# One GAT layer of a six-layer graph network: its last, half-wide block multiplied in the usual way, a mask fetched behind a transposing DMA, and sums of values made over three blocks

## The chip, the cores and the metric

The kernel runs on one core of a Trainium2 chip. The metric is the device time of one execution in microseconds; the median of several runs is compared. A time below 2259.1 us would be faster by more than 0.3%.

## What is computed

A graph of N = 3327 nodes with D = 256 features goes through four residual layers, each `x = layernorm(x + gnn(x, adj))`. The last of them is itself three graph-attention (GAT) layers in a row, so the kernel makes six passes over the graph, named "0", "1", "2", "3a", "3b" and "3c". The change is in layer "1" and where layer "0" passes into it. Cut to what matters:

```python
def gat(x, adj, W, a):                       # layer 1
    h = x @ W
    e = (h @ a[:D, 0])[:, None] + (h @ a[D:, 0])[None, :]
    e = where(e > 0, e, 0.01 * e)
    att = softmax(where(adj > 0, e, -1e12), axis=1)
    return elu(att @ h)

x = layernorm(x + cosine_attention(x, adj))      # layer 0
x = layernorm(x + gat(x, adj, W, a))             # layer 1
x = layernorm(x + dot_attention(x, adj))         # layer 2
x = layernorm(x + gat3(x, adj))                  # layer 3: 3a, 3b, 3c
```

All arithmetic is in float32; `adj` is 0 or 1, about one entry in a hundred, and is turned into a byte mask once.

## The kernel before

**Tiles and blocks.** The nodes are padded to 3328 = 26 tiles of 128 (NT = 26). The target nodes of a pass are cut into seven blocks (NB = 7): six of 512 and a last one, block 6, of 256. In a pass the kernel runs over the blocks `b`, and in a block over the 26 source tiles `j`. For each `(b, j)` it makes the weights `e` (128 source nodes x 512 or 256 targets): ScalarE (ACT) computes a rectified form `re` (L788, four buffers, so that the `re` four tiles on waits until `e` has read this one), and VectorE (DVE) multiplies it with the mask and writes `e` (L801, nine buffers, which the sums named below share). TensorE (PE) then multiplies `e` with the values `v` of tile `j`, which carry a column of ones, so that the sum of weights comes out with the product.

**Two ways to multiply.** The usual way is `plain` (L912 to L919): for each 128 target nodes one product 128 x 257 per source tile, accumulated in a PSUM bank. The other way takes two source tiles as a pair `p` (13 pairs) and two column tiles, and makes seven half-wide products instead of eight, Strassen's scheme in Winograd's form. It needs sums of the weights, `half_sums` (DVE, L901 to L904, four operations for a pair), and sums of the values, `tsums`. In layer 1 block 0 is all plain; in a block for which `half(L, b)` holds, column tiles 2 and 3 are plain and 0 and 1 go through `half_products` (L937); at the end `half_joined` (L953 to L963) puts the seven accumulators together. Block 6 has two column tiles only, and there all products are `half_products`.

**Sums of values.** They don't depend on the block. `combine(key, p, v)` (L837 to L860) makes them for one pair, once a layer: a column of ones by GpSimd (L850), four DVE operations (L851, L852, L858, L859), and a write to DRAM, `t_d` (L860). For each block and pair `fetch_tsum` (L864) brings 256.5 KB back; the buffers, shared by `combine` and `fetch_tsum`, are three. The 13 pairs of layer 1 are made in layer 0's block 6 and in layer 1's blocks 0 and 1, at steps `j` written out by hand; pair 12 is made when its values are done.

**The end of a block.** `finish(L, b, pos)` (L1187) normalizes the accumulators into `p4` (`ri` by DVE L1285 and L1286, the scaling by ACT L1271; for the columns of `half_joined` after the join), turns `p4` and projects it with W, adds the residual and normalizes to `o`. A second turn, of the `o` of the block before, gives the transposed features `ft` that the next layer needs. Both go through `turn` (L1063 to L1081), a generator that runs beside the next block's products: two ACT copies to `planes` (L1070), a transposing DMA on SyncE (SP; L1073), and, some steps later, two copies from `turned` to the place wanted (L1080). So in layer 1 each block has two turns: first `ft`'s, at the block's start, then `p4`'s.

**What sets the order.** The layers are written as a stream of steps, and the framework's scheduler arranges the instructions of each engine for itself, within the data dependences and buffers; the only order asked for by hand is `tc.issue_after(instruction)`, which makes what is issued inside wait in order behind that instruction. SP issues the loads and stores, and its transfers share one queue on 16 DMA engines. In that queue are the mask of the next block (`fetch_mask`, L425 to L428, 1664 KB, or 832 KB for block 6; two buffers; asked for at `j == 8`), the `tsums`, the `t_d` writes of the next layer's pairs, the turns and the rows `x_d` of the residual.

## Time and profile before

| | |
|---|---|
| median of 3 runs | 2265.93 us (2261.41 to 2267.34) |
| profiled execution | 2268.84 us, its span 2266.9 us |
| granted TensorE clock, mean | 0.995 |
| PE busy | 2225.6 us, 98% |
| DVE busy | 2011.5 us, 89% |
| ACT busy | 1360.4 us, 60% |
| layer 1's products, block 0 to 6 | from 466 to about 811 us |
| `tsums<-t_d` fetches in the execution | 230 of 256.5 KB |
| `mask<-mask_d` fetches | 30 of 1664 KB (the page's size; the last block's is half) |

Times in the views are microseconds from the start of the span. An engine's row gives busy time and, in the views of waits, what ended its idle time: `PE po L937 <- DMA tsums<-t_d` reads "PE's product at line 937 waited for the transfer of `tsums`". A matmul in float32 shows as two records. The start of the next record of a filled PE comes 0.111 us after a 128-column one and 0.217 us after a 257-column one; where it comes later, PE stalled. The granted clock is what the throttle gave TensorE, 1.00 being full speed.

### The profile page before, as it was taken

What the parts mean: (1) busy time and instruction counts of PE and PEld (TensorE: products, weight loads), DVE (VectorE), ACT (ScalarE), POOL (GpSimd) and SP (SyncE); (2) the same over time, 40 slices, a digit from 0 to 9 for tenths busy, and PEclk for the clock granted to TensorE, in tenths of its full rate; (3) what the DMA queues carried; (4) which work ended last, traced back from release to release, by engine and by line L of the source; (5) the groups of instructions that cost most, each with busy time, mean ns of one, the idle gap of its engine ahead of it and who ended that gap; (6) DMA issues with size and microseconds to landing.
All of it is one profiled execution on the core that took longest, in us unless ns stands there. A gap on an engine that the chain in (4) does not pass through costs nothing.

```text
span 2266.9 us, 43735 instructions
## 1 busy us (share of the span) xinstructions
PE 2225.6 (98%) x15801; PEld 2034.4 (90%) x15801; DVE 2011.5 (89%) x5682; ACT 1360.4 (60%) x2315; POOL 90.9 (4%) x269
## 2 busy tenths in 40 slices
PE   9999999999999899999999999999999999999997
PEld 7788888888989879999999999999999999999997
DVE  7789999978888788988998879999899998899997
ACT  4677777766666534444444445666666665666663
POOL 0000001000000000000000000000000010000000
PEclk9999999999999999999999999999999999999999
DMA  8655655645665642223222254556536556355542
GB/s 283 196 177 169 196 191 190 188 140 133 156 155 136 157 117 82 62 92 91 61 96 72 75 145 146 158 152 162 141 117 163 147 150 166 100 160 160 152 121 57
DMA packets 207964, 318.05 MB, mean 140 GB/s; under 512 B 82829, under 2 KB 115588, under 8 KB 203140
## 3 DMA queue, kind: packets, MB, share of 16 engines
q1 hardware_dynamic: 198836, 307.12, 46.7%
q0 software_dynamic: 8640, 7.87, 2.3%
q8 instruction: 125, 2.05, 0.4%
q14 instruction: 91, 0.75, 0.1%
q10 hardware_dynamic: 272, 0.26, 0.0%
HBM read 248.69 MB, written 41.85 MB: 128 GB/s over the span
## 4 chain that ended last, share of the span: by engine, by line
PE 84%; DVE 7%; DMA 4%; ACT 2%; issue 2%; POOL 0%; SPq 0%; DVEq 0%; ACTq 0%; POOLq 0%
PE po L1016 46%; PE ps L650 10%; PE po L914 9%; PE ps L511 6%; PE po L937 4%; PE pproj L1336 3%; PE ps L687 2%; DVE ft L801 1%; DMA tsums<-t3a_d 1%; PE pv L1434 1%; PE pgq L541 1%; PE pproj L1131 1%; ACT re L788 1%; DMA turned<-planes 1%; PE pk L371 1%
## 5 line engine op out<-in xcount | busy, mean ns | idle before, releaser
L788 ACT ACTIVATE re<-u,nrh,th 128x512 f32<-128x512 f32 (+1 forms) x728 | 534.1, 777 | 220.7 <-DVE ft L801 120.0
L1016 PE MATMUL po<-tsums,qsum 128*128 128x128 f32 (+1 forms) x2520 | 352.4, 276 | 6.3 <-DMA tsums<-t3a_d 1.9
L801 DVE SCALAR_TENSOR_TENSOR ft<-re,rh,mask 128x512 f32<-128x512 f32 x468 | 338.5, 742 | 5.9 <-ACT re L788 5.9
L1016 PEld LDWEIGHTS po<-tsums,qsum 128*128 128x128 f32 x2520 | 315.9, 192 | 8.4 <-issue 3.5
L1016 PE MATMUL po<-tsums,ssum 128*128 128x128 f32 (+1 forms) x2082 | 316.6, 275 | 2.4 <-DVE ssum L892 1.0
L1016 PEld LDWEIGHTS po<-tsums,ssum 128*128 128x128 f32 x2082 | 286.7, 192 | 16.9 <-issue 5.0
L914 PE MATMUL po<-v,e 128*128 128x257 f32 x1248 | 294.9, 381 | 0.8 <-DVE e L525 0.6
L1016 PE MATMUL po<-v,ft 128*128 128x129 f32 x1872 | 286.3, 276 | 0.7 <-DVE ft L801 0.6
L914 PEld LDWEIGHTS po<-v,e 128*128 128x128 f32 x1248 | 229.8, 190 | 38.4 <-issue 7.9
L1016 PEld LDWEIGHTS po<-v,ft 128*128 128x128 f32 x1872 | 252.1, 192 | 5.2 <-DVE ft L801 1.3
L1016 PEld LDWEIGHTS po<-v,e 128*128 128x128 f32 x1196 | 170.1, 191 | 35.9 <-issue 23.7
L801 DVE SCALAR_TENSOR_TENSOR e<-re,rh,mask 128x512 f32<-128x512 f32 (+1 forms) x234 | 151.2, 655 | 40.8 <-PE po L937 17.7
L524 ACT ACTIVATE ex<-ps,rq 128x512 f32<-128x512 f32 (+1 forms) x183 | 118.9, 652 | 114.0 <-PE ps L511 108.9
L1016 PE MATMUL po<-v,e 128*128 128x129 f32 x1196 | 183.1, 275 | 0.0
L496 DVE SCALAR_TENSOR_TENSOR e<-ex,mask 128x512 f32<-128x512 f32 (+1 forms) x182 | 118.1, 650 | 57.0 <-ACT ex L673 30.4
L511 PE MATMUL ps<-ft 128*128 128x512 f32 (+1 forms) x364 | 167.1, 564 | 0.1
L1016 PE MATMUL po<-tsums,ft 128*128 128x128 f32 x936 | 143.4, 276 | 0.1
L525 DVE SCALAR_TENSOR_TENSOR e<-ex,mask 128x512 f32<-128x512 f32 (+1 forms) x183 | 116.0, 641 | 25.4 <-ACT ex L524 24.8
L1016 PE MATMUL po<-v,qsum 128*128 128x128 f32 x840 | 128.6, 276 | 0.0
L1016 PEld LDWEIGHTS po<-tsums,ft 128*128 128x128 f32 x936 | 123.9, 193 | 0.3 <-ACT p L1271 0.3
L467 DVE CUSTOM_DVE_ANT_0 acc<-acc,stage 128x1024 uint16<-128x1024 uint16 (+1 forms) x168 | 108.3, 645 | 12.2 <-DMA stage<-in_adj_a 9.9
L650 PE MATMUL ps<-gsums,ksum 128*128 128x256 f32 x408 | 111.3, 380 | 0.0
(374 smaller groups left out, 4122.5 us busy)
## 6 DMA issues: line engine op xcount, KB each, us to landing
tsums<-t_d SPq DMA_DIRECT2D x230, 256.5 KB
mask<-mask_d SPq DMA_DIRECT2D x30, 1664.0 KB
stage<-in_adj_a SPq DMA_DIRECT2D x78, 512.0 KB
tsums<-t3a_d SPq DMA_DIRECT2D x77, 256.5 KB
tsums<-t3b_d SPq DMA_DIRECT2D x77, 256.5 KB
tsums<-t3c_d SPq DMA_DIRECT2D x77, 256.5 KB
t_d<-tsums SPq DMA_DIRECT2D x39, 256.5 KB
mask_d<-mask SPq DMA_DIRECT2D x6, 1664.0 KB
```

The costliest lines, as they stand in the source:

```text
L467: nc.vector.tensor_tensor(acc, acc, st[:, h * wd : (h + 1) * wd], ALU.add)
L496: nc.vector.scalar_tensor_tensor(e[:, :wd], t_[:, :wd], 0.0, mask(b, j), ALU.add, ALU.mult)
L511: nc.tensor.matmul(ps[:, :wd], FT[j // 4][:, 0, (j % 4) * P : (j % 4 + 1) * P], FT[b][:, 1, :wd], start=True, stop=True,)
L524: nc.scalar.activation(t_[:, c], ps[:, c], AF.Exp, scale=rq[:, j : j + 1])
L525: nc.vector.scalar_tensor_tensor(e[:, c], t_[:, c], 0.0, mask(b, j)[:, c], ALU.add, ALU.mult)
L650: nc.tensor.matmul(out, l, r, start=first, stop=True, skip_group_check=True)
L788: nc.scalar.activation(t_[:, :wd], self.u[b][:, :wd], AF.Relu, bias=self.nrh[:, j : j + 1], scale=self.th[:, j : j + 1],)
L801: nc.vector.scalar_tensor_tensor(e[:, :wd], t_[:, :wd], self.rh[:, j : j + 1], mask(b, j), ALU.add, ALU.mult,)
L914: nc.tensor.matmul(pos[k - k0], e[:, k * P : (k + 1) * P], v[i], start=(i == 0), stop=(i == NT - 1),)
L937: nc.tensor.matmul(pos[g][:, c : c + n], *m[k], start=(p == 0 and k in (1, 7)), stop=(p == NT // 2 - 1 and k in (5, 3)),)
L1016: nc.tensor.matmul(o, x, y, start=(p == 0 and g not in banks[:i]), stop=(p == NT // 2 - 1 and g not in banks[i + 1 :]),)
L1336: nc.tensor.matmul(pm[:, :D], pT[:, h, :], w[L.w][:, h, :], start=(h == 0), stop=(h == 1),)
```

## The change

It has three parts. `half` no longer holds for block 6, so that its products are plain, 26 tiles x 2 column tiles, without `half_sums`, `tsums` or `half_joined`. `turn` remembers its last transposing DMA, and in layer 1, for blocks 2 to 6, the mask of the next block is issued behind it on SP. And the `combine`s of layer 1's pairs are placed anew: before, pairs 0 to 4 in layer 0's block 6 (at j = 5, 10, 15, 20, 25), 5 to 9 in layer 1's block 0 (j = 1, 5, 9, 13, 17), and 10 and 11 in block 1 (j = 1, 5); after, pairs 0 to 2 in layer 0's block 6 (j = 6, 12, 18), 3 to 8 in block 0 (j = 1 to 21 by four), and 9 to 11 in block 1 (j = 1, 5, 9).

```diff
     def half(L, b):
-        return L.key == "1" and b > 0
+        return L.key == "1" and 0 < b < NB - 1
...
+    last_turn = [None]
+
     def turn(x4, n, out, steps=3, copy=nc.vector.tensor_copy):
...
         tr = work.tile([P, 16, P], U16, tag="stage", name="turned", bufs=4)
-        nc.sync.dma_start_transpose(
+        last_turn[0] = nc.sync.dma_start_transpose(
             out=tr[:, : 4 * n, :], in_=pl[:, :n].rearrange("p k t n -> p (k t n)")
         )
...
         elif j == 8 and not (last and b == NB - 1):
             nb = (b + 1) % NB
-            masks[nb] = fetch_mask(nb)
+            if L.key == "1" and b > 1:
+                with tc.issue_after(last_turn[0].ins):
+                    masks[nb] = fetch_mask(nb)
+            else:
+                masks[nb] = fetch_mask(nb)
...
-        if L.key == "0" and b == NB - 1 and j % 5 == 0 and j > 0:
-            combine("1", j // 5 - 1, V[1])
-        if L.key == "1" and j % 4 == 1 and j < (20, 8, 0, 0, 0, 0, 0)[b]:
-            combine("1", (5 if b == 0 else 10) + j // 4, V[1])
+        if L.key == "0" and b == NB - 1 and j % 6 == 0 and 0 < j < 24:
+            combine("1", j // 6 - 1, V[1])
+        if L.key == "1" and j % 4 == 1 and j < (24, 12, 0, 0, 0, 0, 0)[b]:
+            combine("1", (3 if b == 0 else 9) + j // 4, V[1])
```

## The prediction

> **What bounds the kernel now.** The page comes first: what is busy, and on which line the chain that ended last runs.

> ```profile
> PE 2225.6 (98%) x15801; PEld 2034.4 (90%) x15801; DVE 2011.5 (89%) x5682; ACT 1360.4 (60%) x2315; POOL 90.9 (4%) x269
> PE 84%; DVE 7%; DMA 4%; ACT 2%; issue 2%; POOL 0%; SPq 0%; DVEq 0%; ACTq 0%; POOLq 0%
> ```

> TensorE (PE) is the bound; only its work and its stalls count. The table by stages says where it stalls. Its rows are layer 0's block 6, then layer 1's blocks 0 to 6; after each window and its length stands PE's busy time, and the number after the last engine is the granted clock.

> ```profile
> 432.80:466.00 33.20, 32.30 (x146) 26.57 (x145) 31.02 (x130) 26.13 (x57) 1.07 (x8) 1.00 0.54 181
> 466.00:514.50 48.50, 48.50 (x226) 42.04 (x227) 35.41 (x102) 30.42 (x47) 0.41 (x2) 1.00 0.44 123
> 514.50:559.80 45.30, 45.30 (x312) 42.58 (x311) 37.66 (x117) 31.90 (x49) 0.10 (x1) 1.00 0.49 134
> 559.80:611.40 51.60, 49.71 (x333) 46.30 (x332) 44.12 (x145) 34.61 (x52) 3.95 (x6) 1.00 0.66 157
> 611.40:662.10 50.70, 49.69 (x332) 46.29 (x331) 44.04 (x144) 34.64 (x52) 3.62 (x6) 1.00 0.65 158
> 662.10:714.50 52.40, 49.72 (x333) 46.31 (x332) 44.43 (x148) 34.02 (x49) 3.65 (x6) 1.00 0.58 139
> 714.50:765.60 51.10, 49.88 (x332) 46.14 (x331) 43.01 (x147) 33.55 (x54) 3.65 (x6) 1.00 0.59 149
> 765.60:810.70 45.10, 38.08 (x235) 32.71 (x235) 34.97 (x142) 20.00 (x34) 4.20 (x6) 0.92 0.62 156
> ```

> Blocks 0 and 1 stall nowhere. Blocks 2 to 5 have one gap each of 1 to 3 us, block 6 has 7.0 us and a clock of 0.92. The view of waits over layer 1's blocks 1 to 6 names what ended them (total, times, longest):

> ```profile
> PE po L937 <- DMA tsums<-t_d: 7.3, 5, 2.7
> PE po L937 <- DVE ft L1080: 2.9, 1, 2.9
> PE po L937 <- DVE e L801: 2.6, 1, 2.6
> ```

> A seven-product group at a block's start waits for its sums (`tsums`). The SyncE queue at the start of block 2 (559.8) shows why they are late:

> ```profile
> 552.80 0.38 SPq L427 DMA_DIRECT2D mask<-mask_d  x1
> 554.78 5.02 SPq L1073 DMA_TRANSPOSE turned<-planes  x1
> 559.89 6.52 SPq L864 DMA_DIRECT2D tsums<-t_d  x4
> 567.50 1.85 SPq L1073 DMA_TRANSPOSE turned<-planes  x1
> ```

> The turn of the normalized rows (554.78) stands behind 1664 KB of mask, holds SP for 5.02 us (1.85 where no mask is ahead), and `tsums` is issued only after it. Summing PE's start-to-start excess over its steady pitch gives the stalls: 2.16, 1.27, 2.95 and 1.71 us in blocks 2 to 5, 8.1 together. In block 6 they are 3.02, 1.63, 2.75 and 0.28, 7.7 together, and two of them are followed by half clock (third number before the end 0.51 and 0.53):

> ```profile
> 769.10:772.00 2.90, 2.89 (x13) 2.90 (x14) 1.17 (x5) 2.87 (x5) 0.00 (x0) 0.51 0.36 137
> 789.50:792.60 3.10, 3.04 (x13) 2.95 (x14) 0.16 (x1) 0.00 (x0) 0.00 (x0) 0.53 0.78 195
> ```

> They lose 2.90 x 0.49 + 3.10 x 0.47 = 2.9 us. Block 6 thus has 7.7 + 2.9 = 10.6 us to win, blocks 2 to 5 have 8.1.

> **Block 6 plain.** Removed: 13 pairs x 7 products x 2 records at 0.111 us pitch, 20.3 us. Added: 26 tiles x 2 columns x 2 records at 0.2166, 22.5 us (pitches of L937 and L914). PE +2.3. DVE loses 13 x 4 `hsum` operations at 0.2 us pitch, 10 us of the 34.97 above, off the path. SP loses 13 `tsums` fetches, and with them the waits for their landing, all 10.6 us. What is late next: the first product waits for `e` (0.4, an estimate from DVE's queue at 764 to 766); the projections of block 5 stand after 21 plain products and 8 of `pv`, 21 x 0.433 + 8 x 0.433 = 12.6 us, while the turn they need comes 5.9 us after its planes (772.17 to about 778 in this block), which end about S + 8 (S: the block's first PE product), so about 1.1; the norms 0.3. Together 1.8; bounds 0 (planes as early as now, S + 6.5) and 4.1 (the two largest waits of ACT's `pT` and DVE's `psums` for a turn, 2.1 and 2.0). Sum: -10.6 + 2.3 + 1.8 = -6.5 (-8.3 to -4.2).

> The clock row needs a reason, since other stalls cost none: block 2's 2.06 us and block 4's 2.85 were followed by full clock, 3.02 and 2.75 by half. So I charge nothing for new stalls up to 2.1 us, and 1.45 (half of 2.9) for each of 3 us or more. [...]

> **The mask behind the turn (blocks 2 to 5).** In the built order of the changed kernel SP now has: x_d writes, `tsums` of pair 0, turn, `tsums` 1 to 3, the second turn, mask, write of a `combine`d pair of the next layer (`t_d`, L860), `tsums` 4. The first turn has no mask ahead: its copies can start about 4.4 us after its planes (567.46 to 571.82 in block 2). Planes end at 554.75, S - 5.05; so the turned rows are there at S - 0.65, not S + 3.5 as now. The `tsums` stall goes.

> But the scheduler uses this: the two `ft` copies (L1080; ACT 1.34, DVE 0.75) now stand ahead of `ri` (DVE, L1285) and of the two `p<-po` scalings (ACT, L1271) that free PE's accumulators of the block before. Now these run at S - 1.5 to S - 0.2. By hand through the new order: ACT's sixth `re` waits for DVE's `e` of tile 3 (four buffers); `ft` on ACT runs S + 0.65 to S + 1.9; DVE has `ri` at S + 1.6; the first scaling ends at S + 2.35. The plain columns of the new block queue behind it on PE, and the whole PE queue with them: a stall of about 2.0, and 0.2 for the join (L961). Bounds: 0 if DVE's `e` runs a little earlier and `ft` fits in, 2.95 by the largest block-start stall of the trace.

> The later cost: the second turn's planes end at S + 10.3, its packets run S + 11.3 to 14.05, the mask then needs 5.4 us (packets 553.7 to 559.0 in block 2), to S + 19.4; the `t_d` write and `tsums` 4 stand behind it and land at S + 21.7. PE needs them at S + 21.0: 0.8 stall in blocks 2 to 4 (0 to 3.7), none in block 5, whose next mask is half as large. After: 3 x 3.0 + 2.1 = 11.1 against 8.1: +3.0 (bounds -8.1, all stalls gone, and +7).

> The rule against this move is on the record of layer 2: a mask issued at 896.79 held back the write issued at 897.22 until 904.1. So what stands behind a mask on this queue pays for it; the 0.8 above has it in.

> **Sums over three blocks.** The built order has one `combine` fewer on DVE in layer 0's block 6, and two later ones in layer 1's blocks 0 and 1. One is 4 operations, 0.82 us of DVE. In layer 0 PE's own excess is 2.06 us, and DVE waits 1.01 there for a `tsums` buffer: -0.5 (0 to -0.8). In blocks 0 and 1 DVE has 13.1 us free in 48.5 and PE no stall: 0. If that cover were gone, 2 x 0.82 = 1.6.

> **Sum.** -6.5 + 3.0 - 0.5 = -4.0. The profiled execution took 2268.84 (span 2266.9), 2.9 above the median of 2265.93; the difference carries over: 2264.8 in a profile like that one, **2261.9** as a median.

> **The rivals.**
> *A, the stalls really go.* The `ft` copies find their data ready and cost the path nothing, since the `e` that ACT waits for comes early enough. For: the turn lands before S; DVE is busy 44 of 51 us, so it has room. Against: four copies at the block's narrowest place. The start stalls, 3 x 2.2 + 2.1 = 8.7 us of my 11.1, are gone: 2253.2.
> *B, the mask stalls the middle of the blocks.* One mechanism: in blocks 2 to 4 the planes of the second turn end about 3 us later than S + 10.3 (they queue on ACT behind `re`, which waits for `e`: the 63.1 us of ACT's waits for DVE are mostly that). The mask follows the turn, and `tsums` 4 the mask: stall 3.7, not 0.8. That is 3 x 2.9 = 8.7 more, and half clock after two of three, 2.9: 2273.5 (2270.6 without the clock). It decides from the point where the planes end after S + 12. For: 0.7 us of margin in my chain is the wrong way already. Against: today the planes end at S + 7.7.
> *C, the wait only changes its place.* Whatever is gained at the start is lost to `ri` and the scalings in equal measure; blocks 2 to 5 keep 8.1, the rest holds: 2258.9.

> **How the numbers follow.** Forecast 0.52, own range 2256 to 2267 (its block-start stalls between 0.7 and 3.3 each); A 0.24, B 0.15, C 0.09. 0.3% of 2265.93, about what a measurement of this kernel can tell from no change, is 6.8 us: below 2259.1 or above 2272.7. Faster: 0.3 of the forecast, all of A, half of C: 0.16 + 0.24 + 0.04 = 0.44. Slower: 0.7 of B and 0.02 of the forecast, 0.12. Same 0.44. The range from 2251 to 2272 leaves out the best of A, where everything of the 8.1 goes, and the upper part of B: under 0.2.

> **What would show it.** Block 6: no PE wait for `tsums`, clock 1.00, first product of layer 2 at S + 42 (48.5 now); if it is above S + 44.5, the first term is wrong. Blocks 2 to 5: SP's first turn under 3 us, no mask ahead of it; PE stalled about 2 us at the start by ACT L1271 (two lines further down in the changed file), not by DMA; if that is under 0.5, A. PE's wait for `tsums` at S + 21: 0.8; above 3, B, with rows of half clock. A stall in blocks 0 and 1 would make the last part wrong, and so would a median outside 2251 to 2272.

## The result, and the profile after

The changed kernel takes 2276.86 us (median of 6 runs, 2273.48 to 2282.32) against 2265.39 for the kernel before: a ratio of 1.0052, 95% interval 1.0034 to 1.0070. It is slower by some 11 us; 2261.9 was forecast, and the time lies above the range. The profiled execution took 2274.62 us, one of the changed kernel's faster ones.

The page first: the rows that answer to the two of before.

```profile
PE 2228.3 (98%) x15723; PEld 2030.3 (89%) x15723; DVE 2000.7 (88%) x5623; ACT 1357.2 (60%) x2314; POOL 90.7 (4%) x269
PE 79%; DVE 8%; DMA 8%; ACT 3%; issue 2%; POOL 0%; SPq 0%; DVEq 0%; POOLq 0%; ACTq 0%
```

PE's work is nearly what it was (+2.7 us; +2.3 was forecast for the plain block). But DMA has 8% of the chain that ended last, where it had 4%. The table by stages (layer 0's block 6, then layer 1's blocks 0, 2, 3, 4, 5 and 6) looks for the loss where the change was made:

```profile
432.80:467.10 34.30, 33.18 (x156) 27.61 (x155) 31.01 (x131) 25.73 (x56) 1.17 (x9) 1.00 0.52 168
467.10:515.60 48.50, 48.50 (x226) 41.82 (x225) 35.31 (x101) 30.78 (x47) 0.41 (x2) 1.00 0.45 130
...
561.00:614.00 53.00, 49.88 (x327) 45.61 (x326) 44.18 (x146) 35.00 (x52) 3.96 (x6) 1.00 0.58 152
614.00:666.50 52.50, 50.65 (x338) 46.84 (x338) 43.69 (x145) 34.61 (x52) 3.63 (x6) 1.00 0.57 149
666.50:720.70 54.20, 50.64 (x333) 46.37 (x332) 44.77 (x151) 34.44 (x52) 3.65 (x6) 1.00 0.57 150
720.70:772.30 51.60, 49.60 (x329) 45.61 (x328) 41.89 (x139) 33.58 (x53) 3.84 (x8) 1.00 0.52 125
772.30:811.00 38.70, 37.81 (x159) 29.29 (x158) 28.04 (x104) 19.08 (x35) 3.44 (x4) 1.00 0.66 174
```

Blocks 2 to 5 became longer (53.0, 52.5, 54.2, 51.6 against 51.6, 50.7, 52.4, 51.1). Block 6 lost its gaps and its half clock: 38.7 us at 1.00 instead of 45.1 at 0.92. The two cancel: the first score product of layer 2 starts at 805.6 us, 805.7 before, and layer 2's last score product starts at 1357.7 in both. **The 6 us by which this execution is longer lie behind 1357.7, in layers 3a to 3c and the end of the program, where every engine has the same instructions in the same order.** The stretch from layer 2's last score product to PE's last product is 902.3 us, 896.2 before. What PE waited for in it (total, times, longest), first before, then after:

```profile
PE po L1016 <- DMA tsums<-t3a_d: 1.9, 3, 1.3
...
PE pproj L1336 <- DVE zlast L1511: 1.3, 1, 1.3
PE po L1016 <- DMA tsums<-t3c_d: 1.2, 1, 1.2
...
PE po L1016 <- DMA tsums<-t3b_d: 0.7, 1, 0.7
```

```profile
PE po L1016 <- DMA tsums<-t3a_d: 4.0, 5, 1.7
PE po L1016 <- DMA tsums<-t3b_d: 2.8, 4, 1.7
PE pproj L1338 <- DVE zlast L1513: 2.8, 1, 2.8
...
PE po L1016 <- DMA tsums<-t3c_d: 1.2, 1, 1.2
```

So fetches of value sums in layer 3 land late in a part of the program that was not touched: 8.0 us of waiting for them instead of 3.8. They are not all of it. The piece behind the last product with value sums takes 35.0 us instead of 31.9: there PE waits 2.8 us instead of 1.3 for the last turn (`zlast`), and 3.4 us at half clock follow. That piece is longer (32.9 to 35.0 us against 31.7 to 31.9) in each profile whose stretch is 899 us or more, but for one (r9); how the late fetches lead to it was not traced. The experiments had to tell whether that was chance, and if not, what carries an edit of layer 1 into layer 3.

### The profile page after: what moved, and what is told of

Same layout as the page of the kernel before. It is cut to its first block, busy times and chain, and to the rows that moved or that the text cites. A ratio compares the mean times of both kernels' runs of the same rounds, so it can differ in the third digit from the quotient of the medians.

```text
span 2272.8 us, 43505 instructions
## 1 busy us (share of the span) xinstructions
PE 2228.3 (98%) x15723; PEld 2030.3 (89%) x15723; DVE 2000.7 (88%) x5623; ACT 1357.2 (60%) x2314; POOL 90.7 (4%) x269
## 4 chain that ended last, share of the span: by engine, by line
PE 79%; DVE 8%; DMA 8%; ACT 3%; issue 2%; POOL 0%; SPq 0%; DVEq 0%; POOLq 0%; ACTq 0%
PE po L1016 43%; PE ps L650 10%; PE po L914 9%; PE ps L511 6%; PE pproj L1338 3%; PE po L937 2%; DMA turned<-planes 2%; PE ps L687 2%; DMA tsums<-t3a_d 1%; DMA tsums<-t3b_d 1%; DVE ft L801 1%; DMA tsums<-t_d 1%; PE pgq L541 1%; PE pv L1436 1%; ACT planes L1072 1%
## 5 line engine op out<-in xcount | busy, mean ns | idle before, releaser
L801 DVE SCALAR_TENSOR_TENSOR ft<-re,rh,mask 128x512 f32<-128x512 f32 x468 | 338.7, 742 | 19.2 <-ACT re L788 19.1
L914 PE MATMUL po<-v,e 128*128 128x257 f32 x1352 | 320.4, 381 | 2.9 <-ACT p L1273 2.1
L914 PEld LDWEIGHTS po<-v,e 128*128 128x128 f32 x1352 | 248.9, 190 | 46.3 <-issue 9.8
L1016 PEld LDWEIGHTS po<-v,e 128*128 128x128 f32 x1196 | 170.1, 191 | 36.1 <-issue 23.4
L801 DVE SCALAR_TENSOR_TENSOR e<-re,rh,mask 128x512 f32<-128x512 f32 (+1 forms) x234 | 151.2, 656 | 33.4 <-PE po L937 12.6
L467 DVE CUSTOM_DVE_ANT_0 acc<-acc,stage 128x1024 uint16<-128x1024 uint16 (+1 forms) x168 | 108.4, 645 | 13.2 <-DMA stage<-in_adj_a 11.5
```

The source lines that it names most:

```text
L467: nc.vector.tensor_tensor(acc, acc, st[:, h * wd : (h + 1) * wd], ALU.add)
L801: nc.vector.scalar_tensor_tensor(e[:, :wd], t_[:, :wd], self.rh[:, j : j + 1], mask(b, j), ALU.add, ALU.mult,)
L914: nc.tensor.matmul(pos[k - k0], e[:, k * P : (k + 1) * P], v[i], start=(i == 0), stop=(i == NT - 1),)
L1016: nc.tensor.matmul(o, x, y, start=(p == 0 and g not in banks[:i]), stop=(p == NT // 2 - 1 and g not in banks[i + 1 :]),)
```

## The experiments

Each was timed in five rounds beside the kernel before. "Stretch" is always the time from layer 2's last score product to PE's last product; PE's waits are given as its start-to-start excess over its steady pitch.

**r1: the change once more.** No edit.

> The changed kernel once more, for a second profile. In the first one the end of layer 1 (the first score product of layer 2, ps<-gT,ft) came at 805.6 us, as before (805.7), and the 6 us lost came in layers 3a to 3c, after 1357 us, which the change doesn't touch. Theory 'chance': the stretch behind layer 1 differs by several us between executions of one program; this profile will show it at another length, and the loss in the median must then sit in layer 1 for the most part. Theory 'shifted': something the change leaves behind (13 transfers fewer, another rotation of buffers) makes the stretch from 1357 us to the end longer in every execution: again about 896 to 897 us from the first score product of layer 2's last stretch to the last projection, against 890 before.

Measured: 2278.29 us, ratio 1.0050 (1.0035 to 1.0065). Its profile is of an execution of 2271.01 us, the fastest of six; layer 2 begins at 805.1 and the stretch is 899.2, halfway between 896.2 and 902.3 (the lengths in the expectation are of a shorter piece). The loss of the median is steady, so it isn't chance. Two profiled executions that are both faster than their median can't tell where the rest of it lies; the parts alone can.

**r2, r3, r4: the three parts alone**, each a hunk of the diff on the kernel before.

> Block 6 plain alone, mask and sums as before. Layer 1: blocks 2 to 5 keep their stalls of 8.1 us, block 6 loses its stalls and half clock: first product of layer 2 about 6.5 us earlier (bounds 4.2 to 8.3). If the rest is untouched, ratio about 0.997. Theory 'shifted': the stretch behind layer 1 is 6 us longer here too, since the 13 transfers are gone, and the ratio is about 1.000.

> The mask behind the second turn alone. Theory 'mask' (rival B, smaller): each of blocks 2 to 4 loses about 2 to 3 us to tsums of pairs 4 and 5 behind the mask and 1 to 1.5 at its start, in place of 1.3 to 2.95 before; blocks 2 to 5 together 4 to 6 us longer; block 6, whose first turn has no mask ahead, 2 to 3 us shorter; ratio 1.001 to 1.002. Theory 'shifted' with the loss tied to the mask's order: ratio 1.004 to 1.006, the surplus behind 1357 us.

> The sums of values over three blocks alone. By my sum -0.5 us; by the profile of the changed kernel, where layer 0's block 6 ended no earlier, 0 to +0.5. Ratio 1.000 within 0.001. A ratio above 1.003 would mean that the later write of pair sums is on the path somewhere.

Measured: block 6 plain 2273.22 us, ratio **1.0031** (1.0019 to 1.0043). The mask 2271.98, **1.0028** (1.0019 to 1.0037). The sums 2265.64, 1.0000 (0.9992 to 1.0009).

The sums cost and bring nothing. The mask by itself loses 3.6 us by the first score product of layer 2 (809.3 against 805.7), and its stretch, 895.7, is that of before; the median loses 6.3, more than the 1.001 to 1.002 that was expected. Its waits are not quite those of the whole change, though: its block 6, still with seven-product groups, was expected to be 2 to 3 us shorter and has a stall of 5.6 us of its own (PE's products waiting for DVE's `e`) and 6.8 us at half clock, which the plain block doesn't have.

The plain block is the surprise. Layer 2 begins at 801.2, 4.5 us earlier, at the low end of the forecast's 4.2 to 8.3; and the kernel is 7 us slower, since the stretch is 907.0 instead of 896.2. So the edit that wins in layer 1 loses twice as much in layer 3. PE's waits there:

```profile
PE po L1016 <- DMA tsums<-t3a_d: 7.2, 4, 2.2
...
PE po L1016 <- DMA tsums<-t3c_d: 2.4, 3, 1.2
PE po L1016 <- DMA tsums<-t3b_d: 2.3, 1, 2.3
```

**What differs in layer 3?** The order is the same. Fetch by fetch (231 of them), mostly the same ones are slow in r1, r2 and the changed kernel, and others in the three kernels that keep their half products in block 6 (the fetches' times correlate at 0.75 to 0.83 among the first three, at 0.67 to 0.75 among the others, at 0.34 to 0.43 across). The queues on the page give the clue, before and after:

```profile
q8 instruction: 125, 2.05, 0.4%
```

```profile
q8 instruction: 124, 2.03, 0.4%
```

This is a queue for instructions: 125 packets, 2.05 MB together, 16 KB each, each 1.07 us long in the median (0.96 in the changed kernel). PE ran 15801 products and as many weight loads; with its 416 other records, nearly all waits, that is 32018, or 256 per packet, and the median number of PE's records between two packets is 256 too. So these are pages of PE's program, 256 instructions each. The plain block takes away 39 products of four instructions each and some waits, 164 in all (168 in the whole change). All later page ends are thereby moved by 164 instructions against the work. That gives a theory, 'pages', and a rival, 'buffers': 13 fetches fewer also rotate the three `tsums` buffers.

Counted over layer 3, 27 of the 231 fetches overlap a page's packet in the kernel before (29 in r4, 33 in r3), and 37 in the changed one (36 in r1, 42 in r2). From first packet to last, those that do take 1.8 to 2.2 us in the mean, the others 1.45 to 1.50. Here is one fetch of layer 3b (the row of DMA digits is the busy share of the 16 engines in 40 slices), first in r4, 1804.1 to 1805.5, then the same fetch in r6 (below: the kernel before with its pages moved), 1810.6 to 1813.6:

```profile
DMA  8989998999299499999399989696561313010000
q1 hardware_dynamic: 329, 0.30, 76.8%
```

```profile
DMA  9990599956678885521200100100000940337948
q1 hardware_dynamic: 399, 0.41, 56.5%
q8 instruction: 1, 0.02, 2.4%
```

In the first the busy share falls for good only in the last ten slices, 0.35 us. In the second a page is among the packets, from 1810.72 to 1811.85. Most of the fetch is done by 1812.1, and the digits fall to 2 and 1 and 0; but from 1811.86 to 1813.04 eight of its 128 packets, a sixteenth of the fetch, follow one behind the other, the first as the page ends: by all appearance the share of the page's engine (the trace doesn't name engines). So the fetch's packets take about 2.3 us instead of 1.22.

**r5 to r8: the pages moved by hand.** If that is the cause, giving PE its instructions back must mend it, and taking the same step with the old kernel must break it:

```diff
         def close(self, v, pad=0):
             pm = bank("pmean")
+            for _ in range(pad):
+                nc.tensor.matmul(pm[:1, :1], ones[:, :1], ones[:, :1], start=True, stop=True)
...
+            L.sum.close(nxt[NT - 1], PAD if L.key == "2" else 0)
```

A tiny product is four instructions (two products and two weight loads in the trace: 15847 of each in r6, 15801 in the kernel before). PAD is 41 with the plain block (r5), 23 and 64 with the kernel before (r6, r7), 42 with the whole change (r8).

> Block 6 plain alone, with 41 tiny products (1x1, 164 TensorE instructions) ahead of the mean of layer 2's values, at the beginning of layer 3a. The plain block took about 164 instructions from TensorE's program; these give them back ahead of layer 3. Theory 'pages' (TensorE's program comes in pages of 16 KB, 256 instructions, each a packet of about 1 us on one of the 16 DMA engines; a sums fetch that meets one comes later, and the change moved the pages against the fetches): the stretch from layer 2's last score product to the end of layer 3 goes back from 907 to about 893 to 896 us plus the cost of the 41 themselves (82 records, between 2.5 and 9 us); fetches in layer 3 that meet a page 27 to 33, not 42; ratio 0.998 to 1.001. Theory 'buffers' (another rotation of the three tsums buffers and of the transfers): no change but the cost of the 41; stretch 909 to 916; ratio 1.004 to 1.007.

> The kernel before, with 23 tiny products in the same place (92 instructions), which puts its pages in layer 3 where the plain block's kernel has them. Theory 'pages': stretch behind layer 2 of 900 to 908 us instead of 893 to 896, of which the products themselves are 1.4 to 5; fetches that meet a page about 36 to 42; ratio 1.003 to 1.006. Theory 'buffers': only the cost of the products, ratio 1.0005 to 1.002.

> The kernel before with 64 tiny products in the same place: 256 instructions, one whole page, so the pages in layer 3 stand where they stood. Both theories: only the cost of the 64, 3.8 to 14 us by the bounds; theory 'pages' says that for each product it is less than in the kernel with 23, theory 'buffers' that it is 64/23 of that one's.

> The whole change with 42 tiny products (168 instructions, as many as the change took away). Theory 'pages': stretch behind layer 2 back to 893 to 896 plus the cost of the 42; median 2266 to 2271, ratio 1.000 to 1.0025, what is left being the mask's 3 to 4 us and the cost of the 42 less the plain block's gain. Theory 'buffers': ratio 1.006 to 1.009.

The tiny products themselves cost 2.1, 1.2, 3.3 and 2.2 us of PE's pitch. In the profile of each kernel with them but r6, 3.4 us at half clock come with them or right behind (6.8 in r9 and r10), some 1.6 us more (3.1) that these figures leave out. "Place" is the length of PE's program, four instructions to a product and one to a wait, modulo 256. Only differences of it count, and PE's records in the traces have the same ones (168 and 164 fewer in the change and r2, 93 and 256 more in r6 and r7); layer 3 being the same, it says how the pages stand there.

| kernel | place | median us | ratio (interval) | fetches that meet a page | stretch | PE's wait for `tsums` in it |
|---|---|---|---|---|---|---|
| before | 199 | 2265.4 | | 27 | 896.2 | 4.9 |
| change | 31 | 2276.9 | 1.0052 (1.0034 to 1.0070) | 37 | 902.3 | 9.8 |
| r2 plain block | 35 | 2273.2 | 1.0031 (1.0019 to 1.0043) | 42 | 907.0 | 13.4 |
| r5 plain block + 41 | 200 | 2264.7 | 0.9994 (0.9983 to 1.0006) | 29 | 893.8 | 2.7 |
| r6 before + 23 | 36 | 2281.3 | 1.0080 (1.0065 to 1.0095) | 41 | 907.8 | 13.4 |
| r7 before + 64 | 199 | 2268.6 | 1.0020 (1.0010 to 1.0031) | 26 | 895.3 | 4.0 |
| r8 change + 42 | 200 | 2272.1 | 1.0033 (1.0020 to 1.0046) | 25 | 898.3 | 5.9 |

r6 and r7 settle it. Twenty-three tiny products cost the old kernel 15.8 us, 64 of them 3.2 (2.3 to 7.0 by the interval), about what 64 take: 256 instructions are one page, and the pages stand where they stood. 'Buffers' wanted the larger number to cost more, and falls: neither kernel changes a buffer or a data transfer. The sizes were not all as expected: r6 lost more (ratio 1.0080, 1.006 at most expected), and r8 stayed above its 2271. The waits in layer 3 of r6, then of r7:

```profile
PE po L1016 <- DMA tsums<-t3b_d: 4.8, 4, 2.1
...
PE po L1016 <- DMA tsums<-t3a_d: 4.0, 2, 2.1
...
PE po L1016 <- DMA tsums<-t3c_d: 2.8, 3, 1.5
```

```profile
PE po L1016 <- DMA tsums<-t3c_d: 1.5, 1, 1.5
PE po L1016 <- DMA tsums<-t3a_d: 1.3, 2, 1.1
...
PE po L1016 <- DMA tsums<-t3b_d: 0.6, 1, 0.6
```

And with 41 products *added*, the plain block's kernel gets 8.5 us faster. With its pages in place it is 0.7 us under the kernel before, 2.1 of tiny products included.

Between r5 and r8, both with their pages in place, the mask and the sums cost 7.4 us; the sums alone cost nothing, so that is the mask. Part of it is the clock: in r8's profile each of three stalls of 2.0 us for the sums of pair 4 is followed by 3.4 us at half clock, 1.7 us lost each time. PE's busy time and, third from the end, the granted clock there:

```profile
583.70:587.10 3.40, 3.40 (x14) 3.05 (x13) 2.05 (x6) 1.08 (x2) 0.57 (x1) 0.50 0.45 105
638.30:641.70 3.40, 3.40 (x13) 3.02 (x13) 1.86 (x6) 1.08 (x2) 1.09 (x3) 0.50 0.36 71
692.90:696.30 3.40, 3.40 (x14) 2.94 (x13) 1.80 (x6) 1.08 (x2) 1.03 (x3) 0.50 0.27 40
```

The two profiles of the changed kernel itself have nearly the same stalls and no half clock in layer 1.

**r9 and r10: what of the mask's move is dear.** The SP queue of the changed kernel in block 2 (PE's first product 561.0):

```profile
556.11 1.77 SPq L1075 DMA_TRANSPOSE turned<-planes  x1
...
570.37 1.94 SPq L1075 DMA_TRANSPOSE turned<-planes  x1
572.40 0.93 SPq L427 DMA_DIRECT2D mask<-mask_d  x1
573.44 0.38 SPq L860 DMA_DIRECT2D t_d<-tsums  x1
573.92 9.21 SPq L864 DMA_DIRECT2D tsums<-t_d  x2
```

The first turn takes 1.77 us instead of 5.02, as wanted. The sums of pair 4 are issued at 573.92 behind mask and write, their packets start at 580.43, and PE stalls 1.85 us, until 583.00. At the block's start ACT has the order that the prediction read from the built program:

```profile
560.43 1.34 ACT L1082 COPY ft<-turned 128x1024 uint16<-128x1024 uint16 x1 [0.20 <-DMA turned<-planes]
561.64 0.84 ACT L1273 ACTIVATE p<-po,ri 128x256 f32<-128x256 f32 x2
```

The turned rows are there early, and their copy delays the scalings. PE's waits over layer 1's blocks 1 to 6 of the changed kernel:

```profile
PE po L937 <- DMA tsums<-t_d: 6.7, 5, 1.7
...
PE po L914 <- ACT p L1273: 2.1, 4, 0.9
```

So two things could be undone, on r5's kernel. r9 brings the mask in four pieces behind fetches of sums; r10 also orders the `ft` copies behind the scalings:

```diff
+        if L.key == "1" and 0 < b < NB - 1 and j in (7, 11, 15, 19):
+            ...
+            with tc.issue_after(last_sum[0].ins):
+                nc.sync.dma_start(masks[b + 1][:, c0:c1], mask_d[b + 1][:, c0:c1])
```

```diff
+            if isinstance(copy, tuple):
+                with tc.issue_after(last_norm[t].ins):
+                    copy[t](out(t), trv[:, t])
```

`last_norm` holds the last `p<-po` scaling (for ACT) and the last `ri` (for DVE).

> Block 6 plain with the 41 tiny products (median 2264.7), and the mask of blocks 2 to 6 fetched in four pieces of 416 KB, each behind a fetch of value sums, at j = 7, 11, 15, 19, so that never more than a quarter of it (about 1.4 us of packets) stands ahead of a sums fetch. The order of ft ahead of ri and of the scalings stays as in the changed kernel. Theory 'mask ahead of the sums' (rival B): the stalls for tsums at S + 21 and S + 32 (1.8 and 0.9 to 1.2 in the changed kernel) are gone, those at the start (ACT p, 0.6 to 1.0, DVE p, 0.4) stay; blocks 2 to 5 together 3 to 5 us of stalls instead of 8 to 12; ratio 0.996 to 0.999. If the stalls at S + 21 stay, it was not the mask but the write of pair sums or the turn that held the fetches.

> The same, and the two ft copies put in order behind the two p<-po scalings (ACT) and the last ri (DVE). Theory 'ft ahead of ri': PE's start stalls on ACT p (0.6 to 1.9) are gone, at most the 0.4 on DVE p stays; 1.5 to 4 us less than with the pieces alone; ratio 0.995 to 0.998. If they stay, the accumulators come free late for another reason (ACT's re waiting for DVE's e).

> As the run before, with 21 tiny products instead of 41 (82 records at about 0.026 us, so 1.0 us less): TensorE's pages then stand 80 instructions elsewhere in layer 3, between the good place (199 of 256) and the bad one (31 to 36), at 117. Theory 'pages' gives no sign for a place that wasn't tried: between -1 us (as good as 199) and +13 (as bad as 35) against the run before; in whichever case fetches in layer 3 that meet a page and the stretch behind layer 2 go together: 25 to 30 fetches with 893 to 898 us, 36 to 42 with 899 to 908.

Measured: r9 2268.03 us, ratio 1.0007 (0.9998 to 1.0016). r10 **2257.49, ratio 0.9963 (0.9951 to 0.9976)**. r11 2264.85, 1.0000 (0.9989 to 1.0011).

r9 missed (0.996 to 0.999 was expected). PE's waits for layer 1's sums are gone, as expected. But as much was lost elsewhere: 4.6 us on ACT's scalings at the starts of the blocks, and 5.05 us that were not there before, at the projections around S + 23 (S: the block's first product):

```profile
PE pproj L1134 <- DVE c L1152: 4.6, 3, 2.0
PE po L917 <- ACT p L1276: 3.9, 4, 1.9
```

r10, with the copies in order, has hardly any of either (0.2 us at one projection in blocks 2 to 5), and is 10.5 us faster than r9 where 1.5 to 4 were expected. Blocks 2 to 4, in windows of about a block, PE's busy time being the first number after the length:

```profile
555.00:604.00 49.00, 49.00 (x329) 45.75 (x329) 43.17 (x144) 34.01 (x52) 3.95 (x6) 1.00 0.66 164
604.00:653.50 49.50, 49.50 (x331) 46.02 (x330) 43.48 (x145) 34.23 (x52) 3.62 (x6) 1.00 0.65 161
653.50:704.00 50.50, 50.44 (x335) 46.76 (x334) 44.84 (x151) 34.20 (x53) 3.65 (x6) 1.00 0.64 156
```

Hardly a gap is left. Layer 2 begins at 793.5, 12 us earlier than before. This is what rival A meant, reached with two more edits, and it beats both kernels, by 8 and 19 us, its tiny products included.

r11 is r10 with 20 tiny products fewer, and 7.4 us slower. Its layer 1 is the same (layer 2 at 793.0). Its pages stand at 117, 52 fetches meet one, the stretch is 904.7, and PE's wait for `tsums` in it 10.2 us (r10: 28, 897.0, 4.5). That they go together was right; the bounds for the count, 42 at most, were too low. More meetings than in r6 here cost less, so which fetch is met matters too. r9 and r12, with pages at 197 and 201, have 29 and 26 meetings and stretches of 900.0 and 895.8; r9's has 6.8 us at half clock behind its tiny products in it, r12's 3.4.

**r12: is the order enough?** The whole change with 42 tiny products, the mask as the change has it, only the copies put in order.

> The whole change with 42 tiny products (r8: 2272.1), and only the order of the copies mended: ft behind the scalings and ri, the mask whole and behind the second turn as in the change. Theory 'both are needed': the stalls on ACT p at the start (0.6, 0.6, 0.7, 1.8 in blocks 2 to 5) and on DVE p go, 4 to 5 us, the three of 2.0 at S + 21 on the mask stay; median 2265 to 2269. Theory 'the order was all' (the late turn made the mask late, and with planes ready earlier the mask is through before the sums are needed): the stalls at S + 21 go below 0.5 as well; median 2257 to 2261, as with the pieces.

Measured: 2264.61 us, ratio 1.0003 (0.9993 to 1.0013), 7.5 less than r8. Its profile, of its fastest execution, has no half clock in layer 1. The three stalls of 2.0 at the sums of pair 4 are down to 0, 0.34 and 0.64, so they came for the most part with the late scalings, not from the mask's place alone. But 4.95 us stay at the projections, as in r9:

```profile
PE pproj L1138 <- DVE c L1156: 4.3, 4, 1.5
...
PE po L937 <- DMA tsums<-t_d: 0.7, 2, 0.5
```

The truth lies between the two theories: the order alone brings back what the mask's move cost, and order and pieces together bring the gain. Why the projections wait for `c` in r9 and r12 and not in r10 was not followed up.

## Why the prediction was wrong

**The step that failed** first of all is one that it never wrote down: that everything behind layer 1 runs as before. All its terms are of layers 0 and 1, and there the first profile has -0.1 where -4.0 was forecast (1.2 us are lost by 411 us, ahead of the change), the difference being the mask's. What layer 3 loses by its pages stood at nothing in the sum. By the medians it is 6.9 us in this change (against r8, tiny products taken off), 10.6 in r2 (against r5) and 14.6 in r6, which moves the pages and nothing else. With the mask's 7.4, less the 2.8 that the plain block's kernel gains with its pages in place (r5), that makes the median's 11.5. Counting the 1.6 us at half clock behind the tiny products of r5 and r8 too, the pages are 8.5 and the plain block's gain 4.4. So of the 15 us by which the forecast is too low, about half is the pages; the rest is the mask and what the plain block's gain falls short.

**Block 6 plain: right in layer 1, not in the median.** -6.5 was forecast; from the block 5 product at 738 us to layer 2's first the kernel goes from +6.8 to -0.1, -6.9, and r2, r5 and r8 give -5.6 to -6.9. The clock is 1.00, and no wait for `tsums` is left. Layer 2's first weighted product comes at S + 41.6, as the sign of it said (42), and of the 1.8 charged for new waits 1.4 came: 0.4 at the start, 0.7 at block 5's projections (for which its own terms give 1.3 rather than 1.1) and 0.3 at the norms. What the working missed is that 39 products fewer also are 156 instructions fewer. Why r5's median shows 2.8 to 4.4 us of the 6.5 stays open.

**The mask: the mechanism right, the sizes not.** +3.0 was forecast; from 466 to 738 us the profile gives 6.8 - 1.3 = +5.5, and the medians +7.4. The start stall was put at 2.2 in each block and is 1.0, 0.4, 1.2 and 1.0. The stall behind the mask was put at 0.8 and is 1.85, 1.76 and 1.81; the sums landed when the working said (S + 22.0 against S + 21.7), but PE came for them at S + 20, being less delayed at the start. A second of 0.9 and 1.2 at pair 5 and one of 1.3 at block 5's projections were not in it. That is rival B's mechanism, but with planes as early as assumed, and at half its price for the stall. B gave 2273.5, the nearest to the result, for half of the right reason; that it came so near is luck, since it has nothing of layer 3.

**The sums: right** within what can be measured, -0.5 against 0.0 (r4). **Clock: right in one profile, wrong as a rule.** No stall of the changed kernel's layer 1, the longest 1.9 us, brought half clock, as charged. But r8 has the same layer 1, and its three stalls of 2.0 us did; and block 2's stall of 2.06 us, after which the prediction saw full clock, is 2.05 us in r5, which has the same block 2, and half clock follows (at 564.9). So the same stall brings half clock in one execution and not in another, and charging nothing up to 2.1 us was too little.

**Rival A** was possible after all, but not in this program: the copies at the block's start had to be kept behind the scalings.

## What to carry to other kernels

Here an edit that took 164 instructions out of TensorE's program (r2) moved the program's pages against all later fetches, and that cost 10.6 us, more than the 4.5 by which layer 2 began earlier. So time each edit once more with a few idle products added (23 to 64 of them cost 1.2 to 3.3 us themselves), and compare the time up to the end of the edited stage before you blame the edit. And when a transfer is made earlier, look at what the scheduler then puts first: a copy that is ready early may stand ahead of the work that frees the accumulators, as ACT's of 1.34 us did here ahead of the scalings.
